# Unread products in TensorE's long waits, pooling one operation at a time, and measured durations in the account that orders a fused attention kernel

## The chip, the cores and the metric

One core of one Trainium2 chip. The metric is the time of one execution in device microseconds (us). All runs quoted were of the fast state. Executions of one program mostly agree within about 0.3%; those of e4_onlyfill and e12_pool_margin spread over 0.45%.

## The reference

Two layers on eight images of 256 channels and 32 x 32 points, in float32:

```python
x = x + conv_attention(group_norm(x))   # layer 0: keys and values from the image and from
                                        # three pooled copies of it (16x16, 11x11, 5x5), each with
                                        # a 3x3 depthwise convolution; 8 heads, 1426 keys
t = tokens(x)
t = t + attention(layer_norm(t))        # layer 1: one head of 256
t = t + experts(layer_norm(t))          # 8 experts of three products each
```

What matters here is the pooling of layer 0 (sums over rows and columns of the normalised image) and that the first attention, the second attention and the preparation of the next image all run at once.

## The kernel before

The first 2046 us are the two attentions. The kernel emits the score products of layer 0 step by step and fills the time between with background threads. What runs when is decided while the program is built: an account (`Flow`) holds a modelled time for each engine and each tile, and a thread goes on when its engine, its inputs and a PSUM tile (a buffer that TensorE's products write) are free in the account. Each engine then executes in the emitted order.

```python
AHEAD = {"DVE": 4.0, "ACT": 2.0, "POOL": 4.0, "SP": 10.0}   # how far an engine may run ahead of TensorE
NEAR = {"DVE": 1.5, "ACT": 2.0, "POOL": 1.5, "SP": 10.0}

class Flow:
    def cost(self, engine, op, out, ins):                   # cut: modelled durations, us
        if engine == "PE":
            c = max(0.2, 0.00169 * n)
            return c / 4 + 0.05 if ins[0].shape[0] <= DH or ins[0].shape[1] <= DH else c
        if engine == "ACT":
            return 0.2 + 0.00087 * n
        ...
        return 0.15 + 0.00107 * n
    def runnable(self, need, rank=0):                       # cut
        now = self.now[engine]
        return now <= pe + AHEAD[engine] if at <= now + 0.3 else at <= pe + NEAR[engine]

def small():            # a PSUM tile for any background product: two "sm" and one "sx" in all
    if f.also and f.free("sx") < min(map(f.end, f.slots.get("sm", [None]))):
        return T(psum, [P, 512], "sx")
    return T(shared, [P, 512], "sm", bufs=2)

def add(kc, pt, into):  # adds one probability tile onto another by DMA, issued on GpSimd; frees pt
    f.pool.dma_start(out=..., in_=..., accum_op=ALU.add)

def pool_levels(xi, xl):                                    # cut
    for k in range(2):
        yield pool(xi)                  # one question to the account, then three operations
        t2 = T(work, [P, 32, 16], "pool")
        f.pool.tensor_tensor(t2, one[:, :, 0::2], one[:, :, 1::2], ALU.add)
        f.pool.tensor_tensor(l2, t2[:, 0::2, :], t2[:, 1::2, :], ALU.add)
        f.pool.tensor_scalar(l2, l2, 0.25, 1.0, ALU.mult, ALU.mult)
        yield pool(xi)                  # one question, then seven operations
        ...
    for i, (a, e) in enumerate(ends):
        yield ve(xi)                    # on VectorE; writes t5, a buffer shared with t2 and t3
        f.ve.tensor_reduce(t5[:, :, :, i], img[:, :, :, a:e], AX.X, ALU.add)
```

Names in the profile: `sc` scores, `pt` probabilities, `pv` their product with the values, `sm`/`sx` the small PSUM tiles, `xi` the image, `xl` its pooled copies, `con` the constants, `xr` a piece of the residual. A tap is one of the nine terms of a 3x3 convolution; a site is a place where unread products are put.

Of the kernel before, what the change touches and what calls it, by code (L numbers as in the profile page):

```python
# [16 lines left out]
P = 128  # L17
C = 256
HW = 1024
HEADS = 8  # L20
DH = 32
# [10 lines left out]
CAP = (1.5, 1.5)  # L32
NEVER = 1e9
MARGIN = 1.5
AHEAD = {"DVE": 4.0, "ACT": 2.0, "POOL": 4.0, "SP": 10.0}
NEAR = {"DVE": 1.5, "ACT": 2.0, "POOL": 1.5, "SP": 10.0}
BUFS = {"sm": 2, "sx": 1}
PACE2 = 8.0
LANDING = 9.5
NBOUND = 64  # L40
# [615 lines left out]
class Flow:  # L656
# [4 lines left out]
    class Engine:  # L661
# [3 lines left out]
        def __getattr__(self, op):  # L665
            fn = getattr(self.eng, op)

            def call(*args, **kwargs):
                ins = fn(*args, **kwargs)  # L669
                self.flow.note(self.name, op, ins, args, kwargs)  # L670
                return ins

            return call

    def __init__(self, tc, kit):
        nc = tc.nc
        self.tc, self.kit = tc, kit
        self.now = dict.fromkeys(("PE", "DVE", "ACT", "POOL", "SP"), 0.0)
        self.last = {}
        self.ready, self.read, self.writer, self.reader, self.slots, self.open = {}, {}, {}, {}, {}, set()  # L680
        self.pe = self.Engine(self, "PE", nc.tensor)
        self.ve = self.Engine(self, "DVE", nc.vector)
        self.act = self.Engine(self, "ACT", nc.scalar)
        self.pool = self.Engine(self, "POOL", nc.gpsimd)
        self.sp = self.Engine(self, "SP", nc.sync)
        self.threads = []
        self.cut = {}
        self.also = {}
        self.credit, self.port = [0.0, 0.0], 0.0

    def tile(self, pool, shape, tag, bufs=1):
# [18 lines left out]
    def cost(self, engine, op, out, ins):  # L710
        n = 1
        for s in (out.shape if op != "bn_stats" else ins[0].shape)[1:]:
            n *= s
        if op == "tensor_reduce":
            n = 1
            for s in ins[0].shape[1:]:
                n *= s
        if "dma" in op:
            return 1.0 if engine == "POOL" else 0.4
        if engine == "PE":  # L720
            if op == "transpose":
                return 0.13
            c = max(0.2, 0.00169 * n)
            return c / 4 + 0.05 if ins[0].shape[0] <= DH or ins[0].shape[1] <= DH else c
        psum = any(i.space == PSUM for i in ins)
        if engine == "ACT":
            return 0.2 + 0.00087 * n
        if engine == "POOL":
            if n <= 64 and op == "tensor_tensor":
                return 0.3 + 0.17 * n if n <= NKC else 0.3  # L730
            return 0.15 + (0.0023 if op == "tensor_tensor" else 0.0015) * n
        if op == "reciprocal":
            return 0.1 + 0.0064 * n
        if op in ("tensor_scalar", "tensor_copy") and not psum:
            return 0.14 + 0.00065 * n
        return 0.15 + 0.00107 * n

    def note(self, engine, op, ins, args, kwargs):
        aps = [a for a in (*args, *kwargs.values()) if hasattr(a, "tensor") or hasattr(a, "space")]
        out = kwargs.get("out", args[0] if args else aps[0])  # L740
        srcs = [a for a in aps if a is not out]
        prev = self.last.get(engine)
        if prev is not None:
            self.tc.add_manual_dep(
                ins.ins,
                prev,
                mybir.DependencyInfo(mybir.DependencyClass.NoSync, mybir.DependencyReason.DATA),
                reason="program order",
            )
        self.last[engine] = ins.ins.name  # L750
        start = self.now[engine]
        names = [n for a in srcs for n in self.keys(a)]
        outs = self.keys(out)
        for n in (*names, *outs):
            if self.writer.get(n) != engine:
                start = max(start, self.ready.get(n, 0.0))
        for o in outs:
            if self.reader.get(o, engine) != engine:
                start = max(start, self.read.get(o, 0.0))
        cost = self.cost(engine, op, out, srcs)  # L760

        wide = [a for a in srcs if a.space != PSUM and a.free_size() > 4]
        if "dma" not in op and engine == "POOL" or engine == "DVE" and wide and (len(wide) > 1 or op in ("tensor_scalar", "tensor_copy")):
            start = max(start, self.port)
            self.port = start + cost
        self.now[engine] = end = start + cost
        lag = 0.15
        if "dma" in op:
            lag = 3.0 if engine == "SP" else LANDING
        for n in {*outs, self.key(out)}:  # L770
            self.ready[n] = max(self.ready.get(n, 0.0), end + lag)
            self.writer[n] = "DMA" if "dma" in op else engine
        self.open.difference_update(names)
        for n in {*names, *map(self.key, srcs)}:
            self.read[n] = max(self.read.get(n, 0.0), end + lag)
            self.reader[n] = engine

    @staticmethod
    def key(a):
# [85 lines left out]
def attention(tc, kit, f, outer, ended, nb, consts, x, t1, t2, hn, bounds, vecs, q_t, kv_t, proj_t, gqk_t, wqk, wqkv, vecs1, w1_d, w1c, gate_d, wrc, vecs2, bnvec):  # L865
# [6 lines left out]
    with ExitStack() as ctx:  # L872
# [5 lines left out]
        def T(pool, shape, tag, bufs=1):  # L878
            return f.tile(pool, shape, tag, bufs=bufs)

        def small():
# [3 lines that stand above are left out]

        f.also["sm"] = "sx"
        f.slots["sx"] = [None]

        def load_x(b):
            xi = T(work, [P, 2, HW], "xi")  # L890
# [21 lines left out]
        con = kit.con  # L912
# [122 lines left out]
        turn = [-1]  # L1035
# [5 lines left out]
        def ve(*tiles):  # L1041
            return "DVE", tiles, None
# [4 lines left out]
        def pool(*tiles):  # L1047
            return "POOL", tiles, None
# [224 lines left out]
        def pool_levels(xi, xl):  # L1273

            img = xi.rearrange("p k (h w) -> p k h w", h=32)

            def level(s):
                n = SIDES[s]
                return xl[:, :, OFFS[s] - HW : OFFS[s] - HW + n * n].rearrange("p k (h w) -> p k h w", h=n)

            for k in range(2):
                one, l2, l3 = img[:, k], level(1)[:, k], level(2)[:, k]

                yield pool(xi)
                t2 = T(work, [P, 32, 16], "pool")
                f.pool.tensor_tensor(t2, one[:, :, 0::2], one[:, :, 1::2], ALU.add)
                f.pool.tensor_tensor(l2, t2[:, 0::2, :], t2[:, 1::2, :], ALU.add)
                f.pool.tensor_scalar(l2, l2, 0.25, 1.0, ALU.mult, ALU.mult)

                yield pool(xi)  # L1290
                t3 = T(work, [P, 32, 11], "pool")
                f.pool.tensor_tensor(t3, one[:, :, 0::3], one[:, :, 1::3], ALU.add)
                f.pool.tensor_tensor(t3[:, :, 0:10], t3[:, :, 0:10], one[:, :, 2::3], ALU.add)
                f.pool.tensor_tensor(t3[:, :, 1:11], t3[:, :, 1:11], one[:, :, 2::3], ALU.add)
                f.pool.tensor_tensor(l3, t3[:, 0::3, :], t3[:, 1::3, :], ALU.add)
                f.pool.tensor_tensor(l3[:, 0:10, :], l3[:, 0:10, :], t3[:, 2::3, :], ALU.add)
                f.pool.tensor_tensor(l3[:, 1:11, :], l3[:, 1:11, :], t3[:, 2::3, :], ALU.add)
                flat = xl[:, k, OFFS[2] - HW : OFFS[3] - HW]
                f.pool.tensor_tensor(flat, flat, con[:, K_S11 : K_S11 + 121], ALU.mult)

            t5 = T(work, [P, 2, 32, 5], "pool")
            ends = [(i * 32 // 5, -(-(i + 1) * 32 // 5)) for i in range(5)]
            for i, (a, e) in enumerate(ends):
                yield ve(xi)
                f.ve.tensor_reduce(t5[:, :, :, i], img[:, :, :, a:e], AX.X, ALU.add)
            yield ve(t5, xl)
            l5 = level(3)
            for i, (a, e) in enumerate(ends):
                f.ve.tensor_reduce(
                    l5[:, :, i, :], t5[:, :, a:e, :].rearrange("p k h w -> p k w h"), AX.X, ALU.add  # L1310
                )
            flat = xl[:, :, OFFS[3] - HW :]
            f.ve.tensor_tensor(flat, flat, con[:, None, K_S5 : K_S5 + 25].to_broadcast([P, 2, 25]), ALU.mult)
            pooled.append(True)
# [473 lines left out]
        for i in range(len(steps) + 1):  # L1788
# [26 lines left out]
            if i < len(steps):  # L1815
                f.step((PACE, PACE1))
        f.finish(lambda: projected[0] == nb)
        f.also.clear()
        f.finish(lambda: f.free("sx") < NEVER)

# [623 lines left out]
```

## Time and profile before

| | before |
|---|---|
| time | 3456.7 us (median of 3 runs, 3454.8 to 3458.4) |
| TensorE busy, mean clock | 93%, 0.972 |
| from the start to the first product of the experts | 2055.9 us, of which TensorE is idle 214.0 |
| from there to TensorE's last product | 1384.8 us |

The idle time is the length less TensorE's busy time in the window. The prediction shows the lines of the page, of the stages and of the waits. One more line matters later, from the waits of VectorE (who waited for whom: us in total, times, longest us):

```profile
DVE pool L669 <- POOL xl L669: 54.5, 7, 13.8
```

VectorE stands still 54.5 us because a reduction into the shared pooling buffer was emitted before GpSimd was done with it.

### The profile page before, as it was taken

How to read it: one execution, taken by the hardware profiler on the slowest of the kernel's cores; microseconds unless marked ns; L12 is line 12 of the kernel's file. 1: busy time of each engine (PE TensorE's matmuls, PEld its weight loads, DVE VectorE, ACT ScalarE, POOL GpSimd, SP SyncE). 2: the span in 40 equal slices, each digit the busy share in tenths (PEclk: the TensorE clock that was granted, in tenths of full speed). 3: DMA queues.
4: the chain of work that ended last, by engine and by line, in shares of the span. 5: the costliest groups of instructions: out<-in, count | busy, mean ns of one | idle time of the engine just before them, and what ended most of it. 6: DMA issues, size and time to landing. Idle time of an engine off the chain costs nothing.

```text
span 3452.0 us, 39939 instructions
## 1 busy us (share of the span) xinstructions
PE 3212.7 (93%) x15276; PEld 1785.8 (52%) x15276; DVE 2286.3 (66%) x3922; ACT 1673.9 (48%) x2195; POOL 496.1 (14%) x616
## 2 busy tenths in 40 slices
PE   7788889979989899999989989999999999999998
PEld 3322234425434344434434446746777777777776
DVE  6686877787888788787654534316776666666665
ACT  3566666556666566566655533342223333333332
POOL 2113131131141221321121200004000000000000
PEclk9789999999999999999999999999999999999999
DMA  1346655554554565655565754124430001000000
GB/s 48 75 102 155 144 117 111 131 132 98 137 128 101 127 135 130 137 128 121 117 143 128 150 158 164 61 79 141 140 122 19 19 19 37 19 19 19 19 13 20
DMA packets 103881, 333.28 MB, mean 97 GB/s; under 512 B 12848, under 2 KB 38200, under 8 KB 80448
## 3 DMA queue, kind: packets, MB, share of 16 engines
q0 software_dynamic: 24576, 172.51, 25.5%
q1 hardware_dynamic: 75744, 156.16, 13.2%
q8 instruction: 122, 2.00, 0.2%
q10 hardware_dynamic: 3360, 1.97, 0.2%
q14 instruction: 79, 0.65, 0.1%
HBM read 96.23 MB, written 61.87 MB: 46 GB/s over the span
## 4 chain that ended last, share of the span: by engine, by line
PE 73%; DVE 10%; DMA 6%; ACT 5%; issue 3%; POOL 2%; ACTq 0%; SPq 0%; POOLq 0%; DVEq 0%
PE bank L669 24%; PE sm L669 17%; PE y L669 11%; PE sc L669 8%; PE sx L669 6%; PE pv L669 6%; ACT pt L669 4%; DVE acc L669 4%; DMA pt<-pt 3%; DVE pt L669 1%; DVE rec L669 1%; DMA hn<-pool 1%; DMA t<-xr 1%; POOL pool L669 1%; DMA xr<-in_x_dram 1%
## 5 line engine op out<-in xcount | busy, mean ns | idle before, releaser
L669 ACT ACTIVATE pt<-sc 128x2048 f32<-128x2048 f32 (+1 forms) x384 | 720.4, 1876 | 348.0 <-PE sc L669 258.4
L669 PE MATMUL sc<-q,kn 32*128 32x512 f32 (+1 forms) x3072 | 458.3, 667 | 124.2 <-ACT pt L669 123.1
L669 DVE SCALAR_TENSOR_TENSOR acc<-p,vec,acc 128x225 f32<-128x225 f32 (+7 forms) x928 | 530.4, 578 | 39.6 <-ACT acc L669 14.9
L669 PE MATMUL bank<-h,w2e 128*128 128x512 f32 x1024 | 478.4, 593 | 0.0
L669 ACT ACTIVATE h<-bank,bnvec 128x512 f32<-128x512 f32 x298 | 229.5, 771 | 481.6 <-PE bank L669 481.6
L669 DVE TENSOR_TENSOR pt<-pt,pt 128x1024 f32<-128x1024 f32 x320 | 384.7, 1246 | 85.1 <-DMA pt<-pt 68.4
L669 PE MATMUL pv<-pt,vt 128*32 128x512 f32 (+1 forms) x3072 | 424.4, 625 | 0.0
L669 ACT ACTIVATE h<-c,bnvec 128x512 f32<-128x512 f32 x214 | 162.5, 807 | 323.2 <-DVE c L669 323.2
L669 POOL DMA_DIRECT2D pt<-pt x192 | 169.3, 882 | 975.8 <-ACT pt L669 833.5
L669 PEld LDWEIGHTS sc<-q,kn 32*128 32x128 f32 (+1 forms) x3072 | 119.1, 183 | 315.8 <-ACT pt L669 214.2
L669 DVE TENSOR_TENSOR c<-p1c,bank 128x512 f32<-128x512 f32 x107 | 73.5, 687 | 313.7 <-PE bank L669 313.7
L669 PEld LDWEIGHTS bank<-h,w2e 128*128 128x128 f32 x1024 | 194.5, 190 | 150.6 <-issue 138.1
L669 PEld LDWEIGHTS pv<-pt,vt 128*32 128x32 f32 (+1 forms) x3072 | 61.3, 109 | 311.1 <-issue 299.0
L669 POOL TENSOR_TENSOR rstd<-rstd,mhalf 128x4 f32<-128x4 f32 (+2 forms) x88 | 107.4, 1221 | 714.4 <-DVE rstd L669 586.0
L669 DVE TENSOR_TENSOR h<-h,gates 128x1024 f32<-128x1024 f32 x128 | 157.4, 1230 | 66.3 <-DMA h<-h 59.0
L669 PE MATMUL bank<-hn,w1e 128*128 128x256 f32 (+1 forms) x596 | 188.8, 446 | 10.2 <-DMA hn<-hn 10.2
L669 PE MATMUL y<-t,s3e 128*128 128x256 f32 x768 | 187.8, 381 | 0.0
L669 PE MATMUL sm<-p,v 128*128 128x256 f32 x800 | 187.0, 385 | 0.5 <-ACT sm L669 0.5
L669 PE MATMUL sm<-y,t 128*128 128x256 f32 x720 | 171.9, 385 | 6.6 <-ACT p L669 2.1
L669 PEld LDWEIGHTS sm<-p,v 128*128 128x128 f32 x800 | 149.8, 191 | 48.3 <-issue 27.7
L669 ACT ACTIVATE p<-sm 128x512 f32<-128x512 f32 (+1 forms) x149 | 87.0, 585 | 168.1 <-PE sm L669 134.8
L669 PEld LDWEIGHTS bank<-hn,w1e 128*128 128x128 f32 x596 | 114.0, 193 | 96.5 <-issue 89.7
(294 smaller groups left out, 4606.0 us busy)
## 6 DMA issues: line engine op xcount, KB each, us to landing
pt<-pt POOLq DMA_DIRECT2D x160, 1024.0 KB, 7.2
h<-h SPq DMA_DIRECT2D x72, 512.0 KB, 4.1
xi<-in_x_dram SPq DMA_DIRECT2D x16, 512.0 KB, 4.7
t<-t SPq DMA_DIRECT2D x8, 1024.0 KB, 7.8
res<-t SPq DMA_DIRECT2D x32, 256.0 KB, 4.7
t<-res SPq DMA_DIRECT2D x32, 256.0 KB, 3.1
hn<-res SPq DMA_DIRECT2D x32, 256.0 KB, 3.0
hn<-hn SPq DMA_DIRECT2D x16, 512.0 KB, 5.4
```

Of the source, the lines that this page charges most:

```text
L669: ins = fn(*args, **kwargs)
```

## The change

Three intents. Where the account sees TensorE wait 1.6 us or more, products of constants that nobody reads keep it busy, so that its clock does not fall. The pooling on GpSimd asks the account before each operation, so that it does not stand as a block ahead of the DMA that frees a probability tile. The modelled durations are replaced by measured ones.

```diff
-AHEAD = {"DVE": 4.0, "ACT": 2.0, "POOL": 4.0, "SP": 10.0}
-NEAR = {"DVE": 1.5, "ACT": 2.0, "POOL": 1.5, "SP": 10.0}
+AHEAD = {"DVE": 4.0, "ACT": 2.0, "POOL": 1.0, "SP": 10.0}
+NEAR = {"DVE": 1.5, "ACT": 2.0, "POOL": 1.0, "SP": 10.0}
+WAIT, SPARE = 1.6, 1.0
@@ durations
-            return c / 4 + 0.05 if ins[0].shape[0] <= DH or ins[0].shape[1] <= DH else c
+            return c if self.tiling(ins) is None else c / 4
-            return 0.2 + 0.00087 * n
+            return 0.15 + 0.00084 * n + 0.16 * any(i.free_size() == 1 for i in ins[1:])
+        if op == "scalar_tensor_tensor":
+            return 0.23 + 0.00103 * n
@@ and 0.09 to 0.2 us where TensorE changes between whole and tiled products (cut)
@@ unread products, asked for ahead of each instruction of TensorE (cut)
+    def keep_warm(self, args, kwargs):
+        start = max(...)                # when the account lets the next product start
+        now = max(now, self.free("sm" if "sc" in self.slots else "pv"))
+        if start - now < WAIT:
+            return
+        self.warmer(int((start - now - SPARE) / 0.43))
+        def warm(count):
+            ps = small() if turn[0] >= 0 else T(psum, [P, 512], "pv")
+            for _ in range(count):
+                f.pe.matmul(ps[:, :C], lhsT=kit.ident, rhs=con[:, :C], start=True, stop=True)
@@ pooling (three of seven such lines; one ahead of nearly every operation)
+                yield pool(t2)
                 f.pool.tensor_tensor(l2, t2[:, 0::2, :], t2[:, 1::2, :], ALU.add)
+                yield pool(t2)
                 f.pool.tensor_scalar(l2, l2, 0.25, 1.0, ALU.mult, ALU.mult)
-                yield ve(xi)
+                yield ve(xi, t5)
                 f.ve.tensor_reduce(t5[:, :, :, i], img[:, :, :, a:e], AX.X, ALU.add)
```

More of the change, by code (lines that the diff above doesn't have):

```diff
@@ L668, in call @@
             def call(*args, **kwargs):
+                if self.name == "PE":
+                    self.flow.keep_warm(args, kwargs)
                 ins = fn(*args, **kwargs)
@@ L679, in __init__ @@
         self.last = {}
+        self.warmer, self.warming = None, False
         self.ready, self.read, self.writer, self.reader, self.slots, self.open = {}, {}, {}, {}, {}, set()
@@ L688, in __init__ @@
         self.also = {}
+        self.tiled = None
         self.credit, self.port = [0.0, 0.0], 0.0
@@ L736, in cost, with tiling @@
         return 0.15 + 0.00107 * n
+    @staticmethod
+    def tiling(ins):
+        rows, columns = ins[0].shape[0], ins[0].shape[-1]
+        return "columns" if columns <= DH and rows > 8 else "rows" if rows == DH else None
     def note(self, engine, op, ins, args, kwargs):
@@ L760, in note @@
         cost = self.cost(engine, op, out, srcs)
+        if engine == "PE":
+            tiling = None if op == "transpose" else self.tiling(srcs)
+            if tiling != self.tiled:
+                cost += {None: 0.09, "rows": 0.2, "columns": 0.13}[tiling]
+                self.tiled = tiling
         wide = [a for a in srcs if a.space != PSUM and a.free_size() > 4]
@@ L776, in note @@
             self.reader[n] = engine
+    def keep_warm(self, args, kwargs):
+        if self.warmer is None or self.warming:
+            return
+        aps = [a for a in (*args, *kwargs.values()) if hasattr(a, "tensor") or hasattr(a, "space")]
+        out, now = kwargs.get("out", args[0] if args else aps[0]), self.now["PE"]
+        start = max(
+            [self.ready.get(n, 0.0) for a in aps for n in self.keys(a) if self.writer.get(n) != "PE"]
+            + [self.read.get(n, 0.0) for n in self.keys(out) if self.reader.get(n) != "PE"],
+            default=0.0,
+        )
+        now = max(now, self.free("sm" if "sc" in self.slots else "pv"))
+        if start - now < WAIT:
+            return
+        self.warming = True
+        self.warmer(int((start - now - SPARE) / 0.43))
+        self.warming = False
     @staticmethod
@@ L887, in attention @@
         f.slots["sx"] = [None]
+        def warm(count):
+            ps = small() if turn[0] >= 0 else T(psum, [P, 512], "pv")
+            for _ in range(count):
+                f.pe.matmul(ps[:, :C], lhsT=kit.ident, rhs=con[:, :C], start=True, stop=True)
+            f.open.discard(ps.name)
+            f.read[ps.name] = f.now["PE"]
+        f.warmer = warm
         def load_x(b):
@@ L1292, in pool_levels @@
                 f.pool.tensor_tensor(t3, one[:, :, 0::3], one[:, :, 1::3], ALU.add)
+                yield pool(t3)
                 f.pool.tensor_tensor(t3[:, :, 0:10], t3[:, :, 0:10], one[:, :, 2::3], ALU.add)
+                yield pool(t3)
                 f.pool.tensor_tensor(t3[:, :, 1:11], t3[:, :, 1:11], one[:, :, 2::3], ALU.add)
+                yield pool(t3)
                 f.pool.tensor_tensor(l3, t3[:, 0::3, :], t3[:, 1::3, :], ALU.add)
                 f.pool.tensor_tensor(l3[:, 0:10, :], l3[:, 0:10, :], t3[:, 2::3, :], ALU.add)
+                yield pool(t3)
                 f.pool.tensor_tensor(l3[:, 1:11, :], l3[:, 1:11, :], t3[:, 2::3, :], ALU.add)
@@ L1817, in attention @@
         f.finish(lambda: projected[0] == nb)
+        f.warmer = None
         f.also.clear()
```

## The prediction

> **What bounds the kernel now.** I read the page first, then a table of windows by stage, then the waits of TensorE and ScalarE, then the timelines around the longest waits.
>
> ```profile
> PE 3212.7 (93%) x15276; PEld 1785.8 (52%) x15276; DVE 2286.3 (66%) x3922; ACT 1673.9 (48%) x2195; POOL 496.1 (14%) x616
> PEclk9789999999999999999999999999999999999999
> PE 73%; DVE 10%; DMA 6%; ACT 5%; issue 3%; POOL 2%; ACTq 0%; SPq 0%; POOLq 0%; DVEq 0%
> ...
> 0.00:103.00 103.00, 70.17 (x196) 35.72 (x200) 66.34 (x158) 40.04 (x83) 33.49 (x57) 0.88 0.13 40
> 103.00:350.00 247.00, 196.83 (x1104) 74.24 (x1096) 177.57 (x371) 151.28 (x178) 54.50 (x62) 0.88 0.54 120
> 350.00:2046.00 1696.00, 1574.93 (x8882) 710.29 (x8874) 1258.87 (x2155) 1027.19 (x1219) 350.82 (x415) 0.98 0.57 126
> 2046.00:3452.00 1406.00, 1370.77 (x5106) 965.51 (x5106) 783.51 (x1241) 455.37 (x716) 57.25 (x83) 0.99 0.17 61
> ...
> PE sc L669 <- ACT pt L669: 123.1, 97, 12.6
> ...
> ACT pt L669 <- DMA pt<-pt: 60.1, 17, 12.8
> ```
>
> TensorE is the bound: 93% busy and 73% of the chain that ended last. The rows of the table give length, then busy time of TensorE, weight loads, VectorE, ScalarE and GpSimd, then clock. The experts (from 2046 us) are 97% busy and use almost nothing that the change touches. What can be won lies before: 32.8 us of TensorE idle up to 103 us, 50.2 up to 350, 121.1 up to 2046, together 204. The clock adds to it. A mean of 0.972 with a low state of one half is 2 x 0.028 x 3452 = 193 us at half speed; by the rows about 25, 59, 68 and 28 us. Half speed costs only where TensorE works then.
>
> The largest single cause that I can see is on GpSimd. It sums the image for the pooling and also issues the DMA that adds one probability tile onto another and so frees it. The timelines of GpSimd, ScalarE and TensorE near 510 us:
>
> ```profile
> 501.03 1.03 POOL L669 TENSOR_TENSOR pool<-xi 128x512 f32<-128x512 f32 x1
> ...
> 510.05 0.44 POOL L669 TENSOR_TENSOR xl<-xl,con 128x121 f32<-128x121 f32 x1
> 510.63 0.93 POOL L669 DMA_DIRECT2D pt<-pt  x1
> 511.32 1.32 POOL L669 TENSOR_TENSOR pool<-xi 128x512 f32<-128x512 f32 x1
> ...
> 518.47 0.40 POOL L669 TENSOR_TENSOR xl<-xl,con 128x121 f32<-128x121 f32 x1
> 518.97 0.90 POOL L669 DMA_DIRECT2D pt<-pt  x1
> ...
> 526.20 1.88 ACT L669 ACTIVATE pt<-sc 128x2048 f32<-128x2048 f32 x1 [6.35 <-DMA pt<-pt]
> ...
> 528.13 2.09 PE L669 MATMUL sc<-q,kn 32*128 32x512 f32 x8 [4.28 <-ACT pt L669]
> ```
>
> Ten pooling operations (8 to 10 us) stand as one block ahead of an add, ten more ahead of the next. The exponential then finds no free buffer, and the score products wait for it. The chain is pooling, add, landing (median 7.1 us), exponential, scores. Near 734 us the same pattern gives the longest wait of all, 12.56 us.
>
> **What the Trainium skill says.** "TensorE: Matmul & The Clock Gate", part 1, "What's actually happening": the array runs at half clock until it has been busy for a window of some 3.4 us, and falls back after an idle window. The trace agrees: the first image products took 3.64 us for four instructions and later ones of the same shape 1.88, and the low-clock stretches come in multiples of 3.4 us. The same page, "Architectural detail", says that GpSimd's queue is strictly in order and that TensorE's matmuls are too; so an add waits behind pooling, and a useful product waits behind an unread one. The timeline above agrees for GpSimd.
>
> **The change part by part.**
>
> Unread products. In the instruction order of the built program I count 16 sites with 21, 4, 31 and 15 products before the first score product, and 12, 3, 4, 2, 2, 7, 2, 2, 3, 3, 3, 2 later: 116 in all, of 128x256. A 512-wide pair here takes 0.86 us (8 instructions in 3.60 us, two per product), so a 256-wide one takes about 0.43 us warm and 0.86 cold. That is 50 us of added TensorE time, most of it meant for waits. Three sites can be set against the trace:
>
> ```profile
> 10.29 0.59 PE L669 MATMUL sm<-mv,con 128*128 128x2 f32 x2 [10.29 <-DVE mv L669]
> 14.19 3.64 PE L669 MATMUL sx<-xi,kvw 128*128 128x512 f32 x4 [1.89 <-DVE xi L669]
> 90.69 1.95 PE L669 MATMUL sx<-con,kt 128*128 128x128 f32 x4 [14.29 <-ACT kt L669]
> 99.61 2.81 PE L669 MATMUL sm<-con,kt 128*128 128x128 f32 x8 [4.40 <-ACT kt L669]
> ```
>
> The 21 read the constants, whose DMA is issued at 0.73 us and lands 5.0 us later, so they start near 5.8. With 5 us of cold clock (about 6 of them) and 15 x 0.43 = 6.5 us warm they end near 17, while the product behind them was wanted at 10.29: 6 to 7 us late. The warm image products give some 2 us back. Net about +4.5 us, on the path to the first scores. The 31 take 13.3 us in a wait of 14.3: they fit, and the transposes after it (1.95 us against 0.66 for the same shape warm) save some 2 to 3 us. The 15 take 6.5 us in a wait of 4.4: about 2 us late, paid back by the score and transpose products after it (2.81 and 2.09 us, warm about 1.2 and 1.14). The 12 take 5.2 us before a product that waited 2.68: up to +2. The small sites of 2 to 7 stand before score products that mostly waited 1 to 6 us: about -2 together. Sum of the fillers: +4.5 - 2.5 + 0 + 2 - 2, about +2 us.
>
> Pooling one at a time. In the instruction order, the blocks 10+10 per image between adds become, image by image, 10/1/5/4, 4/7/4/0/5, 2/1/8/7/2, 11/2/7, 1/2/8/3/6 and 3/3/8/6. Blocks are smaller, not gone; an operation is now placed only where GpSimd runs at most 1 us ahead of TensorE in the account, so one left in front of a ready add should cost 1 to 2 us, not 8 to 10. TensorE waits that I put to pooling blocks: 1.8 (near 328), 2.08 + 2.70 + 4.28 (505 to 528), 12.56 (734), 2.45 + 1.23 (967 to 974): 27.1 us. The cold stretches that follow them add up to 41.0 us, with 26.55 us of TensorE work in them by the windows, of which half, 13 us, is lost. I take 85% of 40: -34 us.
>
> VectorE starts. Two taps of the first image are now ahead of the reductions that waited 13.84 us for a pooling buffer: 2 x 1.2 us, about -2.5.
>
> Measured durations. The emission follows the account, so nearly everything before 2046 us is reordered (up to some 40 background products earlier around the sixteenth unit, none by the end). The work is the same. Of the 204 us idle, about 155 remain after the parts above; better costs for ScalarE, for the taps and for the change between tiled and whole products should place some of it better, above all adds that wait behind a reciprocal root on GpSimd that itself waits for VectorE. I allow -6 us, a choice, with 20 us either way because a reordering moves waits as well as removing them.
>
> Sum: +2 - 34 - 2.5 - 6, about -40 us, to 3416 us (-1.2%).
>
> **The rivals.** (1) The unread products are late in practice, because the account's times are not the chip's. Each one issued while something useful is ready delays it in full: at worst 50 us less the real waits, and the start shows it can happen. With pooling gaining only half, the time would be about 3450. For it: the 21 and the 12. Against it: 46 of 116 stand in waits of 14.3 and 4.4 us that are real. (2) The gain of pooling comes back as another wait: later pooled columns delay the maps and the taps on VectorE, 74% busy between 350 and 2046. Then 3430 to 3440. Against it: the adds also feed VectorE (68.4 us of waiting for them in its waits), so it gains too. (3) The account is now so much nearer the chip that half of the remaining idle goes, with its cold clock: 3416 - 60, below 3370. For it: 204 us are there. Against it: part is a dependency of the start that no order removes, and score products in the thin stretches wait about 1.0 us per step for an exponential of 1.88 us with one buffer of scores.
>
> **Range and chances.** 3416 in the middle; the reordering's 20 us and some 15 us on the pooling give about 25 as one deviation, hence 3382 to 3446. Over 2% faster means under 3388, which needs rival 3 in good part: 0.15. Over 2% slower means over 3526, which no rival reaches: 0.02. Else 0.83.
>
> **What would show it.** After the change: the first product with mv should start near 17 us, not 10.3, and the clock be full from about 11 us; no block of ten pooling operations directly ahead of a ready add, and ScalarE's wait for the adds' DMA well below 60.1 us (I expect 20 to 30); no 12.56 us wait near 734; TensorE's wait of scores for the exponential from 123.1 to about 90; mean clock from 0.972 to about 0.982; expert stage within 5 us of 1406 us. I am wrong if the adds are as late as before (then pooling was not what held them), or if the stage from 350 to 2046 us does not shrink by 25 us or more.

## The result, and the profile after

3416.8 us (median of 4 runs, 3414.6 to 3420.3) against 3457.2 in the same rounds. The ratio is 0.9885, 95% interval 0.9868 to 0.9902. A ratio here is the mean time of one kernel's fast runs over that of the other's of the same rounds, so it is not quite the ratio of the medians.

The page of the changed kernel, the lines that answer to those of the prediction:

```profile
PE 3240.7 (95%) x15496; PEld 1818.5 (53%) x15496; DVE 2288.3 (67%) x3914; ACT 1674.6 (49%) x2193; POOL 499.1 (15%) x616
PEclk9899999999999999999999999999999999999999
```

Windows of the kernel before, split at its first product of the experts (length, then busy time of TensorE, weight loads, VectorE, ScalarE, GpSimd, then clock, DMA share, GB/s):

```profile
0.00:2055.90 2055.90, 1841.93 (x10170) 820.29 (x10171) 1504.99 (x2685) 1218.52 (x1479) 438.82 (x533) 0.96 0.54 121
2055.90:3440.70 1384.80, 1370.77 (x5106) 965.48 (x5106) 781.00 (x1236) 455.37 (x716) 57.25 (x83) 1.00 0.17 60
```

The same of the changed kernel:

```profile
0.00:2012.70 2012.70, 1864.50 (x10390) 855.72 (x10391) 1512.65 (x2685) 1217.49 (x1477) 444.76 (x533) 0.98 0.55 124
2012.70:3404.10 1391.40, 1376.19 (x5106) 962.81 (x5106) 775.36 (x1228) 457.06 (x716) 54.37 (x83) 0.99 0.18 63
```

The attentions are 43.2 us shorter, the experts 6.6 longer. TensorE's idle time fell from 214.0 (2055.90 - 1841.93) to 148.2 us. Laying the trace's clock record over TensorE's instructions, its work at half clock in this stage fell from 112.9 to 68.5 us, of which half counts: -22.2. (The record begins at 17.6 us before and at 10.1 us after; 4.5 and 4.3 us of work ahead of it are left out.) All other work rose by 44.8 us, close to the 50 us worked out for the unread products. So -65.8 - 22.2 + 44.8 is the 43.2.

The waits of the changed kernel, from TensorE's, ScalarE's and VectorE's lists:

```profile
PE sc L672 <- ACT pt L672: 102.6, 89, 7.5
...
ACT pt L672 <- DMA pt<-pt: 42.4, 15, 8.2
...
DVE pool L672 <- POOL xl L672: 18.1, 6, 5.5
```

All three are lower (123.1, 60.1 and 54.5 before), and the longest wait of scores is 7.5 in place of 12.6. So the scores' own wait makes up 20.5 of the 65.8 us of idle time that went. VectorE's wait for the adds did not fall: 68.4 us before, 75.1 after. GpSimd's timeline at the same image as in the prediction:

```profile
521.78 0.40 POOL L672 TENSOR_SCALAR xl<-xl 128x256 f32<-128x256 f32 x1
522.17 0.79 POOL L672 TENSOR_TENSOR pool<-xi 128x352 f32<-128x352 f32 x1
522.91 0.94 POOL L672 DMA_DIRECT2D pt<-pt  x1
526.47 1.03 POOL L672 TENSOR_TENSOR rstd<-rstd,mhalf 128x4 f32<-128x4 f32 x1 [2.61 <-DVE rstd L672]
...
531.09 0.44 POOL L672 TENSOR_TENSOR xl<-xl,con 128x121 f32<-128x121 f32 x1
531.49 1.04 POOL L672 TENSOR_TENSOR pool<-xi 128x512 f32<-128x512 f32 x1
532.47 0.90 POOL L672 DMA_DIRECT2D pt<-pt  x1
```

Here four and then seven pooling operations stand between one add and the next, where ten stood (the cut lines hold some of them). Counted over the traces, from the end of the exponential that makes an add ready to the add's issue: adds over 1 us late with pooling in between were 12 before, 87 us late together with up to 10 operations in between; after they are 15, 46 us together, up to 7. Pooling was the smaller part of the lateness, though: another 49 adds before, late by 202 us together, had none in between, mostly a reciprocal root (`rstd` above) that itself waits for VectorE. After, these are 43 adds and 169 us.

The start is where the change loses. TensorE's timeline:

```profile
5.83 11.44 PE L672 MATMUL pv<-con 128*128 128x256 f32 x42 [5.83 <-DMA con<-in_consts_dram]
17.11 0.28 PE L672 MATMUL sm<-mv,con 128*128 128x2 f32 x2
18.23 0.38 PE L672 MATMUL sm<-dev,con 128*128 128x2 f32 x2 [0.84 <-DVE dev L672]
18.47 1.97 PE L672 MATMUL pv<-con 128*128 128x256 f32 x8
20.50 1.98 PE L672 MATMUL sx<-xi,kvw 128*128 128x512 f32 x4
```

The 21 unread products (42 instructions) hold the first useful one until 17.11 us; before, it ran at 10.29. The first scores come at 107.0 us and not at 102.3.

### The profile page after: what moved, and what is told of

Same layout as the page of the kernel before. It is cut to its first block, busy times and chain, and to the rows that moved or that the text cites. A ratio compares the mean times of both kernels' runs of the same rounds, so it can differ in the third digit from the quotient of the medians.

```text
span 3415.2 us, 40385 instructions
## 1 busy us (share of the span) xinstructions
PE 3240.7 (95%) x15496; PEld 1818.5 (53%) x15496; DVE 2288.3 (67%) x3914; ACT 1674.6 (49%) x2193; POOL 499.1 (15%) x616
## 4 chain that ended last, share of the span: by engine, by line
PE 75%; DMA 6%; ACT 4%; DVE 4%; issue 2%; POOL 1%; SPq 0%; ACTq 0%; DVEq 0%; POOLq 0%
PE bank L672 25%; PE sm L672 18%; PE y L672 11%; PE sc L672 8%; PE sx L672 7%; PE pv L672 6%; ACT pt L672 4%; DMA pt<-pt 2%; DMA t<-xr 2%; DMA xr<-in_x_dram 1%; DVE acc L672 1%; DVE pt L672 1%; DVE rec L672 1%; DMA hn<-pool 0%; DMA hn<-hn 0%
## 5 line engine op out<-in xcount | busy, mean ns | idle before, releaser
L672 PE MATMUL sc<-q,kn 32*128 32x512 f32 (+1 forms) x3072 | 448.1, 654 | 103.7 <-ACT pt L672 102.6
L672 DVE TENSOR_TENSOR pt<-pt,pt 128x1024 f32<-128x1024 f32 x320 | 391.5, 1265 | 85.1 <-DMA pt<-pt 75.1
L672 PE MATMUL sm<-p,v 128*128 128x256 f32 x768 | 180.0, 386 | 6.6 <-DVE xr L672 6.6
L672 PE MATMUL sm<-y,t 128*128 128x256 f32 x688 | 163.5, 384 | 2.1 <-ACT p L672 2.1
```

The costliest lines, as they stand in the source:

```text
L672: ins = fn(*args, **kwargs)
```

## The experiments

Theory: the smaller pooling blocks carry nearly all of the gain, the unread products pay for themselves, and the durations add a few us. Rivals: the unread products carry it through the clock; the reordering by new durations carries it; or the sum is the luck of one order. Each run was timed in five rounds against the kernel before; the medians of before were 3456.0 to 3457.4 us. The tables give this kernel's median, its runs and the ratio.

| run | what it is | us | ratio (95%) |
|---|---|---|---|
| e1_nofill | changed, no unread products | 3412.1 | 0.9873 (0.9859 to 0.9888) |
| e2_onlypool | before + pooling part | 3427.4 | 0.9916 (0.9903 to 0.9929) |
| e3_onlycost | before + durations (and one line of pooling) | 3466.8 | 1.0027 (1.0017 to 1.0037) |
| e4_onlyfill | before + unread products | 3485.6 | 1.0074 (1.0061 to 1.0086) |
| e5_oneproduct | e4 with one product at each site | 3481.4 | 1.0077 (1.0063 to 1.0091) |
| e6_t5wait | before + one line of pooling | 3445.7 | 0.9968 (0.9956 to 0.9979) |
| e7_sizedstart | e1 + unread products at the start only | 3413.8 | 0.9869 (0.9855 to 0.9883) |
| e8_pertact | e1, one constant moved by 0.01 us | 3477.1 | 1.0062 (1.0049 to 1.0075) |
| e9_before_act | before, one constant moved by 0.01 us | 3485.5 | 1.0090 (1.0076 to 1.0105) |
| e10_pool_act | e9 + pooling part | 3438.5 | 0.9951 (0.9939 to 0.9964) |
| e11_before_margin | before, margin moved by 0.1 us | 3444.9 | 0.9967 (0.9954 to 0.9980) |
| e12_pool_margin | e11 + pooling part | 3446.7 | 0.9972 (0.9963 to 0.9981) |

**Without the unread products.**

```diff
-        f.warmer = warm
```

> The changed kernel without its 116 unread products; the order of the useful instructions on TensorE, GpSimd and the DMA queue is the same. Theory (the products cost about what they save, +2 us net): 3412 to 3418 us against 3417. Rival (they hold the clock and are a good part of the gain): 3430 us or more, mean clock back near 0.975. In either case the product with mv starts near 10.3 us again and the first scores about 3 us earlier or no later.

3412.1 us: as the theory said, and the rival falls. The clock did fall back as the rival expected (0.974 to 0.977 in the four runs, against 0.980 to 0.984 with the products), but the time did not follow. Built, both programs have the same useful instructions in the same order on every engine; only some small PSUM tiles differ. In the profiled runs the unread products cost 5.0 us (3415.2 against 3410.2). TensorE's timeline without them:

```profile
10.07 0.59 PE L672 MATMUL sm<-mv,con 128*128 128x2 f32 x2 [10.07 <-DVE mv L672]
...
13.97 3.78 PE L672 MATMUL sx<-xi,kvw 128*128 128x512 f32 x4 [1.89 <-DVE xi L672]
...
89.00 1.95 PE L672 MATMUL sx<-con,kt 128*128 128x128 f32 x4 [12.54 <-ACT kt L672]
...
99.57 2.80 PE L672 MATMUL sm<-con,kt 128*128 128x128 f32 x8 [6.26 <-ACT kt L672]
```

The first scores are at 102.3 us again. Up to the experts' first product, idle time is 187.2 us without and 148.2 with them, half-clock work 88.2 and 68.5: the unread products turn 39 us of idle time and 10 us of clock loss into 53 us of work.

**The pooling part alone.** Edit: on the kernel before, all lines of the diff above under "pooling", and 1.0 for GpSimd in `AHEAD` and `NEAR`.

> The kernel before with only the pooling emitted one operation at a time (and GpSimd's lead cut to 1 us). Theory (pooling carries about 34 of the 40 us): 3420 to 3430 us. Rival (the gain comes from the reordering by new durations): 3445 us or more.

3427.4 us, 30 below before: as the theory said. Its waits on TensorE, ScalarE and VectorE:

```profile
PE sc L672 <- ACT pt L672: 114.4, 95, 7.7
...
ACT pt L672 <- DMA pt<-pt: 27.0, 10, 6.2
...
DVE pool L672 <- POOL xl L672: 7.9, 5, 3.1
```

Both waits that the part is aimed at have fallen to less than half, from 60.1 and 54.5 us. The scores' wait at the end of the predicted chain fell only from 123.1 to 114.4, 8.7 of the 30 us.

**The durations alone.** Edit: on the kernel before, the lines of the diff under "durations". Without the one line `yield ve(xi, t5)` this does not build (the scheduler finds a deadlock in the order), so the run has it too.

> The kernel before with only the measured durations in the account (the wait of the reductions for their own tile is kept, without it the program does not build). Theory (-6 us, 20 either way): 3440 to 3460 us. Rival (the durations carry the gain): 3420 to 3430 us.

3466.8 us: 9 us slower, outside the theory's range by a little and against the rival. So the durations carry nothing alone. Against e6_t5wait below, which has that line and the old durations (3445.7), they cost 21. On top of the pooling part they give 15 us (3427.4 to 3412.1). All of this lies within what an order alone is worth (e8 below), so neither the loss nor the gain is shown to be that of the durations.

**The unread products alone.** Edit: on the kernel before, the lines under "unread products".

> The kernel before with only the unread products, placed by the old account. Theory (net zero): 3452 to 3464 us. Rival (the clock): 3440 us or less.

3485.6 us: 28 slower, and both expectations miss. There are again 16 sites, 21, 4, 31 and 14 at the start. The useful order is that of the kernel before, line by line, except for which of the three small PSUM tiles a product writes. The largest single loss against before is near the 248th score step. Before:

```profile
1386.24 1.99 PE L669 MATMUL sx<-xi,qw 128*128 128x512 f32 x4 [1.29 <-DVE xr L669]
```

With the unread products, the same stretch:

```profile
1406.88 3.78 PE L672 MATMUL sm<-xi,qw 128*128 128x512 f32 x4 [7.08 <-DVE xr L672]
```

The product now stands in another tile, whose reader on VectorE waits for a DMA; 1.29 us became 7.08, and its clock fell.

**One product at each site.**

```diff
-            for _ in range(count):
+            if count > 0:
                 f.pe.matmul(ps[:, :C], lhsT=kit.ident, rhs=con[:, :C], start=True, stop=True)
+                for _ in range(count - 1):          # in the account alone
+                    f.now["PE"] += f.cost("PE", "matmul", ps[:, :C], [kit.ident, con[:, :C]])
```

> The kernel before with the unread products of the old account cut to one at each of the 16 sites; order and PSUM tiles are the same as with all of them (3485.6 us). Theory formed from that trace (the loss of 28 us is mostly that the unread products take one of the three small PSUM tiles, so that useful products land in other tiles and wait for other readers): 3470 to 3485 us. Rival (it is TensorE time spent on unread products, some 50 us of which 7 remain): 3464 us or less.

3481.4 us: nearly the whole loss stays with 16 products, some 7 us of work. So the time of the other 90 is not the cause: taking it away, with order and tiles kept, gives back 4 us. Built, this program and the kernel before differ only in the 16 products and in the small PSUM tiles (1281 of 18778 TensorE instructions have another). That leaves the tiles as the likeliest cause; no run moved the tiles without any product. The product of the last two listings still waits in its new tile, and still runs at half clock:

```profile
1401.01 3.78 PE L672 MATMUL sm<-xi,qw 128*128 128x512 f32 x4 [5.06 <-DVE xr L672]
```

In sum the loss shows as clock and not as waiting: idle time up to the experts is about that of before (215.6 against 214.0), half-clock work is up from 112.9 to 142.6 us, of which half counts, 15 us.

**One line of the pooling part.**

```diff
-                yield ve(xi)
+                yield ve(xi, t5)
```

> The kernel before with one line of the pooling part alone: a reduction on VectorE is emitted only when the tile that it writes is free. Theory (in-order VectorE no longer stands 54.5 us behind pooling for that tile, a share of the 30 us that the pooling part gave): 3435 to 3450 us. Rival (only the smaller pooling blocks count): 3452 to 3462 us.

3445.7 us, 10 below before, as the theory said, and VectorE's wait for the pooling buffer fell from 54.5 to 28.9 us. That the 10 us come from that wait is not shown: the line changes the order too, and e11 below gave 11 with nothing of the pooling changed.

**Unread products sized for the start.** Only the sites ahead of the first scores, 5, 4, 31 and 15:

```diff
+            if turn[0] >= 0:
+                return
+            first_site.append(count)
-            for _ in range(count):
+            for _ in range(5 if len(first_site) == 1 else count):
```

> The changed kernel with unread products only before the first scores and the first site cut from 21 to 5, so that they end near 10.3 us; order and PSUM tiles as without any (3412.1 us). Theory (the clock is up for the first image products and after the 14 us wait, nothing is late): first scores 2 to 4 us before 102.3 us, time 3407 to 3411 us. Rival (the wait for VectorE and ScalarE behind takes it back): 3412 to 3416 us.

3413.8 us, in the rival's range. The four runs lie from 3407.5 to 3419.9, so they do not exclude the theory. The profiled one is the slowest; TensorE's timeline in it:

```profile
5.10 4.63 PE L672 MATMUL pv<-con 128*128 128x256 f32 x10 [5.10 <-DMA con<-in_consts_dram]
9.60 0.59 PE L672 MATMUL sm<-mv,con 128*128 128x2 f32 x2
...
15.03 3.11 PE L672 MATMUL sx<-xi,kvw 128*128 128x512 f32 x4
```

The start is on time now, but the first scores are at 102.1 us, 0.2 earlier than without any. Five products were over before the clock rose, at 17.5 us (17.9 without them, 10.1 in the changed kernel). The transposes after the wait of 14 us do run faster, and the wait for ScalarE behind them takes it back.

**Another order of the same quality.** The changed kernel without unread products, and

```diff
-            return 0.15 + 0.00084 * n + ...
+            return 0.16 + 0.00084 * n + ...
```

> The changed kernel without unread products, with one constant of the account moved (0.15 to 0.16 us for a ScalarE instruction): another order of nearly the same quality. Theory (the account's order is worth a few us either way, so part of what parts of the change give together is luck of the order): 3400 to 3430 us, other than 3412 by 5 us or more. Rival (the measured value is what counts): within 4 us of 3412.

3477.1 us: 65 above 3412.1, far more than the theory itself allowed. One hundredth of a us in one constant takes away the whole gain of the change. Windows of this run, split at the experts' first product:

```profile
0.00:2088.80 2088.80, 1860.75 (x10180) 830.49 (x10180) 1520.85 (x2693) 1220.11 (x1480) 448.92 (x535) 0.95 0.54 119
```

and of e1_nofill:

```profile
0.00:2008.80 2008.80, 1821.64 (x10159) 816.13 (x10159) 1512.15 (x2685) 1218.23 (x1477) 445.20 (x533) 0.97 0.56 124
```

Idle time is 228.1 us against 187.2, half-clock work 150.6 against 88.2. The gap grows through the whole stage (9 us at the 60th score step, 36 at the 216th, 80 at the last), at no single place; the experts' stage, with 16 instructions fewer, gives 10 back. Yet only 9 adds are late behind pooling in this run, 23 us together, fewer than in any of the faster runs: that lateness alone does not set the time.

**The kernel before and the pooling part, in two other orders each.** Edits: `0.2 + 0.00087 * n` to `0.21 + 0.00087 * n`, and `MARGIN = 1.5` to `MARGIN = 1.6`, in the kernel before and in e2_onlypool.

> The kernel before with one constant of its account moved by 0.01 us (0.20 to 0.21 for a ScalarE instruction). Theory (an order is worth some tens of us either way whatever the values): away from 3456 by 8 us or more, in either direction. Rival (the order before is as any other of its kind): within 5 us.

> The same 0.01 us moved, with the pooling part alone added. Theory (pooling one at a time removes a real wait, about 30 us in any order): 20 to 40 us below the run with the same constant and the old pooling. Rival (its 30 us were the luck of one order): within 12 us of it, or above.

> The kernel before with another constant of its account moved (the margin from 1.5 to 1.6 us). Theory (luck of the order): away from 3456 by 8 us or more, in either direction. Rival: within 5 us.

> The same margin, with the pooling part alone added. Theory (pooling removes a real wait in any order): 20 to 40 us below the run with the same margin and the old pooling. Rival (luck): within 12 us of it, or above.

3485.5 and 3438.5 us with the first constant: pooling gives 47, more than the theory's 20 to 40. 3444.9 and 3446.7 with the second: it gives nothing (-2), the rival's case. So three orders of the kernel before lie from 3445 to 3486 us, and the theory of luck holds for both. (The runs of e12 alone lie from 3440 to 3456.) Of the pooling part's gain three pairs say 30, 47 and -2 us, 25 in the mean with about 14 of standard error. What it does on GpSimd is the same in all three: adds that pooling made late were late by 87, 89 and 109 us together without it, and by 48, 69 and 48 with it. Whether that becomes time depends on the rest of the order. Little of it goes through the predicted chain: TensorE's wait of scores for the exponential fell by 8.7, 3.6 and 0.2 us in the three pairs. In the third, ScalarE's wait for the adds fell from 61.1 to 34.8 us and no time was gained; in the second, the largest gain, the products that wait for a piece of the residual (`xr`) or for a weight that a DMA brings (`res`) have 28 of the 44 us that TensorE's waits lost.

## Why the prediction was right or wrong

The total was right to 1 us (3416 against 3416.8), and inside the range. Step by step that is better than it deserves, and with orders 65 us apart the hit on the total is luck.

- **The start and the 21 products: right.** "Near 17 us" was 17.11 (the same product ran at 10.07 without the 21, so it does wait behind them), "about +4.5" to the first scores was +4.7, and the clock rose at 10.1 us where "about 11" was said. The sum of the fillers, "about +2", was +5: the gains of the later sites, put at -2.5, did not come. e7 shows why for the 31 and the 15: the wait for ScalarE after them takes the warm clock back. (The "0.86 us" for a pair is not the quotient 3.60 / 4 = 0.90; a 256-wide product measured 13.55 / 31 = 0.44 us, so the 50 us came to 53.)
- **Pooling, "-34" and "-2.5": -30 measured together in this order, -47 and +2 in two others.** The first links of the chain are seen in the traces: the 12.56 us wait is gone, the adds are earlier, ScalarE's wait is shorter. The last link, exponential to scores, gave only 8.7 us, where 27.1 us of waits and 13 of clock were counted on; for the rest the prediction's chain is not shown. "1 to 2 us" of remaining lateness was too hopeful: 46 us over 15 adds is 3. And a part of it may be filed wrongly: the reductions into the shared buffer, put at -2.5 for the start alone, waited at seven places and not at one, and their line alone ran 10 us faster (e6), which would leave 18 us for the smaller blocks.
- **Measured durations, "-6 ... with 20 us either way": the centre cannot be judged, the width was too small.** With pooling they gave 15, without it they cost 9, and another order of the same account lies 65 us away. The step that failed is "I allow -6 us, a choice, with 20 us either way because a reordering moves waits as well as removing them". The mechanism stands, its size does not: orders that differ by one constant (before, e9, e11; e1, e8) span 41 and 65 us.
- **Rival 1, unread products that are late: half right.** It was the products' time that I feared. In this change that time is covered by waits except at the start. Alone they cost 28 us (e4), and not for their time alone (e5).
- **Rivals 2 and 3.** Rival 2, the gain coming back as another wait, is not what the total shows, but its counter-argument failed: VectorE did not gain on the adds, its wait for them rose from 68.4 to 75.1 us. Rival 3 did not come: 148 us of idle time are left up to the experts.
- **Marks that I set.** Mean clock 0.983 for "about 0.982"; ScalarE's wait for the adds 42.4 for "20 to 30"; scores' wait for the exponential 102.6 for "about 90"; experts 6.6 us longer and not within 5. The stage from 350 us to the experts had to shrink by 25 us or more: it did, by 36 (the score step at 349.3 us comes 7.6 us earlier, the experts' first product 43.2).

What stays open: how much of the 40 us is the change and how much is this order. Shown are a time of adds late behind pooling that falls in every order tried (by 23 to 56%) without the scores' wait following it, a mean gain of pooling of 25 us over three pairs, a cost of 5 us for the unread products, and no gain of the durations that would stand out of the spread. The fastest kernel run, e1_nofill, is the change without its unread products; e7 and it are the same within their spread, and the intervals of its ratio and of the change's overlap, so its lead of 5 us is not certain by the times alone; that the first scores come 4.7 us earlier speaks for it.

## What to carry to other kernels

Where a program's order comes from a greedy account, measure a part of a change in several orders (move a constant by a hundredth and rebuild) before believing its few per cent: one order here was worth up to 65 us. An unread product is not free even in a true wait: it needs a PSUM tile, it delays what becomes ready while it runs, and a warm clock pays only where TensorE, and not the engine behind it, sets the pace (0.2 us at the first scores in e7). A slow housekeeping queue that also frees buffers should be asked operation by operation (25 us in the mean of three pairs here, but from -2 to 47); look for the time from "ready" to "issued" of its urgent instructions.

## What the Trainium skill lacked or had wrong

- "TensorE: Matmul & The Clock Gate", "Why this matters for your kernels", advises no idle gaps over some 3 us between bursts of products, so that the clock does not fall. In this kernel shorter ones are enough: the clock record of the kernel before goes to one half at 352.1 us, after a wait of 1.41 us and 0.6 us into one of 1.01 us among score products, and at 304.3 us with a single wait of 1.0 us in the 3.4 us before. The page's "A second HAM failure mode: psum-queue depth-cycling" does say that frequent short idles make the clock fall, but gives no length.

```profile
349.32 1.14 PE L669 MATMUL sc<-q,kn 32*128 32x512 f32 x8 [1.41 <-ACT pt L669]
...
352.46 2.09 PE L669 MATMUL sc<-q,kn 32*128 32x512 f32 x8 [1.01 <-ACT pt L669]
```

- The same page, part 1, says that the ramp costs under 1% of a typical kernel. For the start that holds here: 4.5 us of work at half clock, so some 2 of 3452 us. It is not the whole cost of the clock: with the later falls TensorE worked 127.8 us at half clock, so about 64 us (1.9%) were lost.
- The same page advises to keep TensorE busy. What that costs it doesn't say: 116 unread products took 53 us, saved 39 us of idle time and 10 us of clock, and left 5 us lost; in the profiled run of e7_sizedstart five products of 0.9 us each at the start, with TensorE busy from 5.10 to 10.19 us, did not raise the clock.
- No page has it that a product put in to fill takes a PSUM tile and so moves later products to other tiles: 16 such products, some 7 us, cost 25 us (e5_oneproduct), and 1281 of 18778 instructions changed their tile.
- No page has it how far the time of a program depends on its order alone: 65 us of 3412 for 0.01 us in one constant of the account (e8_pertact).
